# Slot attention and a rounded FFN on one core: a Newton step and the moves of the value states at other places, weight pieces at fixed points

## The chip, the cores and the metric

The kernel runs on one core of a Trainium2 chip. The metric is the device time of one execution in microseconds (us). The engines have short names: PE (TensorE, matmuls and transposes), DVE (VectorE), ACT (ScalarE), POOL (GpSimd) and SP (SyncE, which issues most DMAs). Each engine works through its own queue in order.

## What is computed

Four sequences (b = 0 to 3) of 512 tokens with 512 features go through an attention with slots and then through a feed-forward net (FFN) whose weights are rounded to fp8. Both read a layernormed input and add to the residual stream.

```python
# attention, 16 heads, DK = M = 64, DV = 128
q, k, v = x @ Wq, x @ Wk, x @ Wv                    # per head
s = clip(x @ Ws, -32, 32)                           # 64 slots per head
z = cumlogsumexp(s, axis=time); p = exp(s - z); g = exp(z_before - z)
hk[t] = hk[t-1] * g[t] + k[t] (x) p[t];  ok[t] = (q[t] * DK**-0.5) @ hk[t]
pv = softmax(ok)                                    # over the slots
hv[t] = hv[t-1] * g[t] + p[t] (x) v[t];  o[t] = pv[t] @ hv[t]
o = o * rsqrt(mean(o**2) + eps) * g_norm * silu(x @ Wg)
y = o @ Wo
# FFN, 1536 hidden
h = silu((x @ fp8(gate_w)) * gate_scale) * ((x @ fp8(up_w)) * up_scale)
y = (h @ fp8(down_w)) * down_scale
```

## The kernel before

**Units.** The 16 heads are taken in 8 groups g of two heads. A unit is one group of one sequence, written (g,b). The first 16 units have b = 0 and 1 (for each g first b = 0, then b = 1), the second 16 have b = 2 and 3. Even g also project the values of two groups (ps_v, 48 matmuls), so even units are longer. Where fp32 accuracy is wanted, a matrix is held in three parts (a high part, a low part, a corrected one) and a product is three passes of matmuls: 12 for a 128 x 512 result (L513, L550), 24 in four blocks for the output (L867).

**One unit** (`attention`, L950). On PE: slots ps_s, keys ps_k, queries ps_q; transposes of e (the exponentials of the clamped slot logits) and of k; in even units the values; transposes of the unit before's output (ps_oT, `turn_output`); ps_a (keys by queries within blocks of 64 tokens), ps_sk and ps_sv (states, `key_states` and `value_states`); the two gates ps_g; ps_ok (`slot_scores`, L697); then the unit before's output projection ps_o in shares of 6, 10, 4 and 4 matmuls, between which the softmax runs: transposes ps_okn of okT (L731), transposes ps_w of the exponentials (L775), ps_b (L780), and at last ps_ov (`read_states`, `read_within`). So the unit before's output is scaled, transposed, split and projected inside this one (object `before`).

**Names that the change touches.** z is the running sum of the slots' exponentials and rzT its reciprocal, first as exp(-ln z) on ACT (L661, L662) and then made exact by a Newton step on DVE (`inverse`, L664: L666 and L667). okT = ps_ok times rzT (L727, DVE) and wT = ps_w times rzT (L777, DVE). `turn_output` multiplies the transposed output with the gate (L846, DVE, sg); `high_output` rounds it on ACT (L852), `split_output` makes the other two parts on DVE (L856, L857). States of one half of the partitions are needed in the other half: `key_states` has three POOL operations for that (L685 to L687) and `value_states` four (L761 to L764); ps_ov reads the result, moved_v and svo. POOL's queue also issues the DMAs that add the output's rows to the residual stream in DRAM (L879), behind ACT's copy y of ps_o (L878), and has the small power operations (L339, L821).

**The list of work.** `work` is a Python list of small pieces that the program's author lets issue between a unit's own steps. In the first half these are the splits of the raw weights: ACT makes a high part (L260), DVE the other two (L266, L267), 512 columns at a time; the last piece of a matrix also starts a DMA that keeps it for the second half. A piece's high part is issued one step ahead of its rest. In the second half they are the rounding of the FFN's weights (`quantize`, in steps of two DVE operations each: L457 and L458, L464 and L465, L470 and L471, the last with a DMA). There are also pieces of the layernorm of later sequences (xn, xs). `other(n)` issues n entries (by default pace[0]), `piece()` issues up to the next whole piece, `need(key)` all entries up to the last one named key. `next_step` and `early_step` issue one transposing step of a layernorm. `load` starts the next unit's weights. What is issued where depends on g, b, on pace[0] and on what the list has at its head; `first_unit` writes the order of unit (0,0) out by hand. In ACT's queue, `exp_and_log` loads the table for exponentials and logarithms after the gates' Silu.

The order in which the engines get their instructions is the order of these calls; nothing is moved by a scheduler.

Of the kernel before, what the change touches and what calls it, by code (L numbers as in the profile page):

```python
# [40 lines left out]
AF = mybir.ActivationFunctionType  # L41
# [8 lines left out]
def kernel(  # L50
# [18 lines left out]
    nc = tc.nc  # L69
# [102 lines left out]

    pace = [1]

    def other(count=None):
        for _ in range(count or pace[0]):
            if work:
                work.pop(0)[1]()

# [114 lines left out]
    def next_step():  # L294
        if steps:
            steps.pop(0)()
# [328 lines left out]
    class Heads:  # L625


        def __init__(self, g, b):
            self.u, self.g, self.b = f"{g}_{b}", g, b
            self.v0 = g % 2 * HV  # L630
            self.sg = []
# [123 lines left out]
        def value_states(self):  # L755
            pts = states(self.e, both_v[self.b], self.v0, DV, f"ps_sv_{self.u}")
            self.sv = one.tile([P, NT - 1, DV], F32, tag="sv", name=f"sv_{self.u}")
            self.svo = svo = one.tile([P, NT, DV], F32, tag="svo", name=f"svo_{self.u}")
            add_up(svo, pts, self.sv)
            self.moved_v = moved = one.tile([P, NT, DV], F32, tag="kT", name=f"moved_v_{self.u}")  # L760
            nc.gpsimd.tensor_copy(moved[half(0), 1:, :], self.sv[half(1)])  # L761
            nc.gpsimd.tensor_copy(moved[half(1), 0, :], svo[half(0), 0, :])
            nc.gpsimd.tensor_tensor(moved[half(1), 1:, :], svo[half(0), 1:, :], self.sv[half(0)], ALU.add)
            nc.gpsimd.tensor_tensor(svo[half(1), 1:, :], svo[half(1), 1:, :], self.sv[half(1)], ALU.add)  # L764
# [70 lines left out]

        def gate(self, h):
            self.sg.append(one.tile([P, T], F32, tag=f"sg{h}", name=f"sg_{self.u}_{h}"))
            p = project("g", self.b, f"{'g'}_{self.u}_{h}", h * DV)
            nc.scalar.activation(self.sg[h], p, AF.Silu)

        def turn_output(self, h, n_bank=None):

# [40 lines left out]
    def exp_and_log():  # L883
        nc.scalar.preload_act_table_set("natural_log_exp_and_others")

    def first_unit():
# [11 lines left out]
        for _ in range(5):  # L898
            piece()
        transposing = layernorm(1, 1)  # L900
        work.extend(parts())
        load_matrix("g", 0, True)
        other(2)
        X.slots()
        other(2)
        X.keys()
        X.running_sum()
        other(2)
        X.queries()
        X.turn_e()  # L910
        X.turn_k()
        other(2)
        X.values(2)
        other(2)
        X.key_states()
        X.move_queries()
        X.inverse()
        X.values(3)
        fetch()
        fetch()  # L920
        load_matrix("o", 0, True)
        other(1)
        transposing()
        next_step()
        other(2)
        X.query_key()
        next_step()
        other(3)
        X.gate(0)
        X.slot_scores()  # L930
        X.value_states()
        next_step()
        X.softmax()
        X.softmax_exp()
        other(1)
        X.gate(1)
        exp_and_log()
        X.slot_weights()
        X.move_weights()
        next_step()  # L940
        X.weight_slot()
        need("xs_1")
        X.softmax_sum()
        need("xs_0")
        piece()
        X.read_states()
        X.read_within()
        return X

    def attention(g, b, before, load, gated):  # L950

        X = Heads(g, b)
        even = g % 2 == 0
        small = other if even or b > 1 or pace[0] > 1 else piece
        first = pace[0] > 1 and even and b == 1

        def early_step():

            if not any(name.endswith("_m") for name, _ in work):
                next_step()

        need(f"xs_{b}")
        need("s")
        X.slots()
        load("s")
        if not even:
            early_step()
        before.scale_output()  # L970
        need("k")

        X.keys()
        before.scale_other()
        X.running_sum()
        if not first:
            small()
        load("k")
        if not even:
            early_step()  # L980
        need("q")
        X.queries()
        if first:
            other(3)
        elif even or turned():
            other()
        load("q")
        X.turn_e()
        if even:
            X.turn_k()  # L990
            next_step()
            if turned():
                other(1)
            need("v")
            X.values(0)
            if first or b > 1:
                other(1)
            X.values(1)
            before.turn_output(0)
            before.high_output(0)  # L1000
            before.turn_output(1)
            before.high_output(1)
            other()
            X.values(2)
            before.split_output(0)
            next_step()
            other()
            X.values(3)
            before.split_output(1)
            next_step()  # L1010
        else:
            before.turn_output(0)
            X.turn_k()
            before.turn_output(1)
            before.high_output(0)
            before.high_output(1)
        X.query_key()
        X.key_states()
        X.value_states()
        X.move_queries()  # L1020
        if even:
            other()
        else:
            if b > 1:
                early_step()
            before.split_output(0)
            before.split_output(1)
        X.inverse()
        if work and work[0][0] == "o":
            other()  # L1030
        need("g")
        X.gate(0)
        if even:
            other()
            next_step()
        elif work and work[0][0] == "o":
            other()
        X.gate(1)
        exp_and_log()
# [24 lines left out]
        X.softmax_sum()  # L1064
        X.read_states()
        if even and b == 1 and not first and not turned():
            piece()
        elif even or b > 1 or steps:
            other()
# [105 lines left out]
    with tc.manual_schedule(engines=EVERY):  # L1175
# [17 lines left out]
        for i, (g, b) in enumerate(units[1:], 1):  # L1193
# [13 lines left out]

            def gated():

                pace[0] = 1 + (pace[0] > 1 and i > 1)  # L1210
# [20 lines left out]
            if b > 1:  # L1231
                for _ in range(min(0 if units[i] == (0, 2) else 2 if g % 2 else 4 if b == 2 else 3, to_come[0])):
                    work += [("round", f) for f in quantize()]
                    to_come[0] -= 1
            pace[0] = 2 if i == 1 or (g, b) in ((0, 2), (NG - 1, 0), (NG - 1, 2)) else 1
            if i == 1:
                pass
            elif g % 2:
                if b > 0 and not turned():
                    piece()  # L1240
                while work and work[0][0][:2] in ("xs", "xn") and b % 2:
                    other(1)
# [94 lines left out]
```

## Time and profile before

| | us |
|---|---|
| median of 3 runs | 1437.73 (1436.96 to 1437.81) |
| the profiled execution | 1438.3 |
| its span, first to last instruction | 1436.6 |
| granted TensorE clock, mean | 0.994 of full speed |

| stretch of the span, us | PE busy | DVE busy | ACT busy | POOL busy |
|---|---|---|---|---|
| 0 to 57.8, unit (0,0) | 50.42 | 42.64 | 27.86 | 15.52 |
| 57.8 to 590, rest of the first half | 512.16 | 369.96 | 305.88 | 172.85 |
| 590 to 1121, second half but its last unit | 518.58 | 398.61 | 275.79 | 171.93 |
| 1121 to 1160, unit (7,3) | 35.50 | 26.91 | 20.97 | 11.70 |
| 1160 to 1436.6, FFN | 271.21 | 117.61 | 73.90 | 14.38 |

Such tables are busy time by engine and stretch. Below, lines of a timeline read: start, duration, engine, line, operation, what is written and read, shapes, how many, and in brackets the idle time before it and what ended it. A line of the waits reads: engine and instruction, what it waited for, then the total, the number of waits and the longest one.

### The profile page before, as it was taken

How to read it: one execution, taken by the hardware profiler on the slowest of the kernel's cores; microseconds unless marked ns; L12 is line 12 of the kernel's file. 1: busy time of each engine (PE TensorE's matmuls, PEld its weight loads, DVE VectorE, ACT ScalarE, POOL GpSimd, SP SyncE). 2: the span in 40 equal slices, each digit the busy share in tenths (PEclk: the TensorE clock that was granted, in tenths of full speed). 3: DMA queues.
4: the chain of work that ended last, by engine and by line, in shares of the span. 5: the costliest groups of instructions: out<-in, count | busy, mean ns of one | idle time of the engine just before them, and what ended most of it. 6: DMA issues, size and time to landing. Idle time of an engine off the chain costs nothing.

```text
span 1436.6 us, 31108 instructions
## 1 busy us (share of the span) xinstructions
PE 1387.9 (97%) x13163; PEld 1108.3 (77%) x13163; DVE 955.7 (67%) x1625; ACT 704.4 (49%) x1329; POOL 386.4 (27%) x433
## 2 busy tenths in 40 slices
PE   8999899999999999999999999999999999999998
PEld 4687787778777877778777877877887788888886
DVE  6767657765786578667877887787778753435333
ACT  4556555655665555544545554455545543222221
POOL 2133323322332234332323341243224220000000
PEclk9999999999999999999999999999999999999999
DMA  8174655665565574546546664667465561101000
GB/s 337 67 242 141 184 143 177 185 201 162 164 188 173 153 235 126 140 140 205 170 119 178 213 173 121 184 199 208 109 184 170 154 184 23 59 1 59 0 30 29
DMA packets 80890, 213.04 MB, mean 148 GB/s; under 512 B 6168, under 2 KB 35120, under 8 KB 75568
## 3 DMA queue, kind: packets, MB, share of 16 engines
q1 hardware_dynamic: 62224, 177.49, 33.7%
q0 software_dynamic: 18528, 33.58, 15.7%
q8 instruction: 103, 1.69, 0.5%
q14 instruction: 35, 0.29, 0.1%
HBM read 107.23 MB, written 108.00 MB: 150 GB/s over the span
## 4 chain that ended last, share of the span: by engine, by line
PE 75%; DVE 18%; ACT 4%; issue 2%; POOL 0%; DMA 0%; DVEq 0%; ACTq 0%; POOLq 0%
PE ps_v L550 11%; PE ps_o L867 10%; PE ps_fg L1087 6%; PE ps_fu L1087 6%; PE ps_s L513 5%; PE ps_q L513 5%; PE ps_g L513 5%; PE ps_k L513 5%; PE ps_fd L1148 3%; PE ps_fe L1148 3%; DVE oT L857 2%; DVE sv L621 2%; PE ps_ov L796 2%; DVE z L666 2%; PE ps_ov L806 2%; PE ps_oT L565 2%
## 5 line engine op out<-in xcount | busy, mean ns | idle before, releaser
L867 PE MATMUL ps_o<-w_o,oT 128*128 128x512 f32 x768 | 213.7, 412 | 5.9 <-DVE w_o L267 4.7
L513 PE MATMUL ps_g<-xs,w_g 128*128 128x512 f32 x744 | 181.0, 399 | 0.0
L879 POOL DMA_DIRECT2D stream<-y x128 | 111.9, 874 | 222.1 <-ACT y L878 219.3
L550 PE MATMUL ps_v<-w_v,xs 128*128 128x512 f32 x720 | 171.5, 393 | 0.0
L513 PEld LDWEIGHTS ps_g<-xs,w_g 128*128 128x128 f32 x744 | 138.9, 190 | 33.9 <-issue 5.2
L867 PEld LDWEIGHTS ps_o<-w_o,oT 128*128 128x128 f32 x768 | 134.5, 189 | 36.0 <-DVE w_o L267 5.6
L550 PEld LDWEIGHTS ps_v<-w_v,xs 128*128 128x128 f32 x720 | 132.9, 188 | 26.2
L685 POOL COPY moved<-sk 64x192 f32<-64x192 f32 x32 | 11.2, 350 | 417.3 <-DVE sk L621 417.3
L1108 DVE SCALAR_TENSOR_TENSOR h<-ps_fu,scol,act 128x512 f32<-128x512 f32 x48 | 36.0, 751 | 113.7 <-PE ps_fu L1087 113.7
L846 DVE SCALAR_TENSOR_TENSOR sg<-ps_oT,scol,sg 128x512 f32<-128x512 f32 x64 | 46.4, 748 | 97.3 <-PE ps_oT L565 95.6
L878 ACT COPY y<-ps_o 128x512 f32<-128x512 f32 x128 | 74.5, 582 | 45.5 <-PE ps_o L867 44.8
L1087 PE MATMUL ps_fg<-xs,wf 128*128 128x512 f32 x384 | 95.7, 391 | 0.0
L1087 PE MATMUL ps_fu<-xs,wf 128*128 128x512 f32 x384 | 94.8, 389 | 0.0
L513 PE MATMUL ps_s<-xs,w_s 128*128 128x512 f32 x372 | 93.8, 401 | 0.0
L513 PE MATMUL ps_q<-xs,w_q 128*128 128x512 f32 x372 | 90.1, 391 | 1.6 <-DVE eT L638 1.6
L513 PE MATMUL ps_k<-xs,w_k 128*128 128x512 f32 x372 | 89.6, 390 | 0.0
L557 ACT COPY v<-ps_v 128x512 f32<-128x512 f32 x60 | 35.3, 588 | 102.2 <-PE ps_v L550 102.2
L821 POOL TENSOR_TENSOR rs<-rs,mhalf 128x8 f32<-128x8 f32 x32 | 58.3, 1823 | 99.1 <-DVE rs L818 87.7
L1087 PEld LDWEIGHTS ps_fu<-xs,wf 128*128 128x128 f32 x384 | 72.1, 188 | 15.0
L1087 PEld LDWEIGHTS ps_fg<-xs,wf 128*128 128x128 f32 x384 | 71.5, 188 | 14.9 <-issue 0.2
L513 PEld LDWEIGHTS ps_q<-xs,w_q 128*128 128x128 f32 x372 | 69.4, 188 | 17.1 <-issue 2.8
L513 PEld LDWEIGHTS ps_s<-xs,w_s 128*128 128x128 f32 x372 | 67.7, 189 | 18.0 <-issue 4.3
(168 smaller groups left out, 2870.6 us busy)
## 6 DMA issues: line engine op xcount, KB each, us to landing
stream<-y POOLq DMA_DIRECT2D x128, 256.0 KB, 4.9
split_v<-w_v SPq DMA_DIRECT2D x4, 3072.0 KB, 11.9
split_g<-w_g SPq DMA_DIRECT2D x8, 1536.0 KB, 7.9
split_o<-w_o SPq DMA_DIRECT2D x8, 1536.0 KB, 7.1
w_v<-split_v SPq DMA_DIRECT2D x4, 3072.0 KB, 16.2
w_g<-split_g SPq DMA_DIRECT2D x8, 1536.0 KB, 6.9
w_o<-split_o SPq DMA_DIRECT2D x8, 1536.0 KB, 8.6
rounded<-qw SPq DMA_DIRECT2D x36, 256.0 KB, 4.3
```

The source lines that it names most:

```text
L513: nc.tensor.matmul(p, wt[self.nm][:, j, at : at + P], xs[self.b][i][:, c, :], start=(i == 0 and c == 0), stop=(i == 2 and c == KC - 1),)
L550: nc.tensor.matmul(p, xs[b][i][:, c, n * P : (n + 1) * P], wt["v"][:, j, c * 2 * HV : (c + 1) * 2 * HV], start=(i == 0 and c == 0), stop=( ...
L557: nc.scalar.copy(to, p)
L565: nc.tensor.transpose(pt[:, n, :], s, by)
L821: nc.gpsimd.tensor_tensor(rs, rs, mhalf.rearrange("p (h n) -> p h n", h=HG), ALU.pow)
L846: nc.vector.scalar_tensor_tensor(self.sg[h], pt.rearrange("p n t -> p (n t)"), gw, self.sg[h], ALU.mult, ALU.mult,)
L867: nc.tensor.matmul(self.p, self.oT[:, i, h, n * P : (n + 1) * P], wt["o"][:, j, h * D : (h + 1) * D], start=(i == 0 and h == 0), stop=(i = ...
L878: nc.scalar.copy(y, self.p)
L879: nc.gpsimd.dma_start(stream[self.b][n * P : (n + 1) * P, :], y, accum_op=ALU.add)
L1087: nc.tensor.matmul(pp, w[:, c * P : (c + 1) * P], xs[b][k][:, c, :], start=(c == 0 and k == 0), stop=(c == KC - 1 and k == 1),)
L1108: nc.vector.scalar_tensor_tensor(h, pu, us, act, ALU.mult, ALU.mult)
L1148: nc.tensor.matmul(sums[n], parts[k][:, n * P : (n + 1) * P], fw[c][2], start=(c == 0 and k == 0), stop=(c == NFC - 1 and k == 1),)
```

## The change

It has four parts.

1. `inverse` issues right after the transposes of e (odd units) or of k (even units), before `turn_output`, and no longer after `move_queries`.
2. The four POOL operations of `value_states` become `move_states`, which issues after `slot_scores` and the first six matmuls of the output projection, so behind the first stream DMA on POOL's queue.
3. The pieces of `work` are issued by a new `fill(count)` at fixed places of a unit, the same for all even and all odd units but for b < 2: one whole piece, or one entry in the second half, and then a high part that is at the list's head. The places that depended on pace[0], and the pieces ahead of each unit, go. Unit (0,1) issues the remaining parts of the first sequence's input, xs_0, before its ps_a.
4. In unit (0,0) the slots' clamp, the Newton step and ps_a come earlier, both gates leave PSUM only after ps_b (so that one pair of ACT's table loads goes), and the parts of xs_0 and the split of w_o move to unit (0,1).

PE's, DVE's, POOL's and SP's instructions are the same ones in another order; ACT has two fewer, both loads of a function table. PE's order changes in unit (0,0) alone.

```diff
@@ class Heads
+        def move_states(self):
+            svo = self.svo
             self.moved_v = moved = one.tile([P, NT, DV], F32, tag="kT", name=f"moved_v_{self.u}")
             nc.gpsimd.tensor_copy(moved[half(0), 1:, :], self.sv[half(1)])
...
         def gate(self, h):
-            p = project("g", self.b, f"{'g'}_{self.u}_{h}", h * DV)
-            nc.scalar.activation(self.sg[h], p, AF.Silu)
+            self.pg[h] = project("g", self.b, f"{'g'}_{self.u}_{h}", h * DV)
+        def gate_silu(self, h):
+            nc.scalar.activation(self.sg[h], self.pg.pop(h), AF.Silu)
@@ new
+    def fill(count):
+        for _ in range(count):
+            if pace[0]:
+                piece()
+            else:
+                other(1)
+        if work and work[0][0] in ("s_", "k_", "q_", "g_", "v_", "o_"):
+            other(1)
@@ first_unit
         X.turn_k()
+        X.inverse()
         other(2)
         X.values(2)
         other(2)
+        X.query_key()
         X.key_states()
         X.move_queries()
-        X.inverse()
...
         X.value_states()
+        X.move_states()
...
         X.weight_slot()
+        X.gate_silu(0)
+        X.gate_silu(1)
+        exp_and_log()
         need("xs_1")
         X.softmax_sum()
-        need("xs_0")
-        piece()
         X.read_states()
         X.read_within()
+        work.extend(later)
+        load_matrix("o", 0, True)
@@ attention
+        pace[0] = b < 2
...
         X.running_sum()
-        if not first:
-            small()
         load("k")
...
+        fill(1 if b < 2 else 2)
         need("q")
         X.queries()
-        if first:
-            other(3)
-        elif even or turned():
-            other()
         load("q")
         X.turn_e()
         if even:
             X.turn_k()
+            X.inverse()
             next_step()
-            if turned():
-                other(1)
             need("v")
             X.values(0)
-            if first or b > 1:
-                other(1)
+            fill(1)
             X.values(1)
...
             before.high_output(1)
-            other()
+            fill(1)
             X.values(2)
             before.split_output(0)
             next_step()
-            other()
+            fill(1)
             X.values(3)
             before.split_output(1)
             next_step()
+            fill(1)
         else:
+            X.inverse()
             before.turn_output(0)
...
+        if units[1] == (g, b):
+            need(f"xs_{b - 1}")
         X.query_key()
         X.key_states()
         X.value_states()
         X.move_queries()
-        if even:
-            other()
-        else:
+        if not even:
             if b > 1:
-                early_step()
+                turning(True)
             before.split_output(0)
             before.split_output(1)
-        X.inverse()
-        if work and work[0][0] == "o":
-            other()
+            fill(1)
         need("g")
...
         X.slot_scores()
         before.project_output(6)
+        X.move_states()
         X.softmax()
         X.softmax_exp()
-        if even and b == 1 and not first and not turned():
-            piece()
-        elif not turned():
-            small()
-        elif not even and b > 1:
-            other(1)
+        fill(1)
         before.project_output(10)
...
-        small()
         X.softmax_sum()
+        if even or b > 1:
+            fill(1)
         X.read_states()
-        if even and b == 1 and not first and not turned():
-            piece()
-        elif even or b > 1 or steps:
-            other()
+        fill(1)
@@ the loop over units
-            pace[0] = 2 if i == 1 or (g, b) in ((0, 2), (NG - 1, 0), (NG - 1, 2)) else 1
-            if i == 1:
-                pass
-            elif g % 2:
-                if b > 0 and not turned():
-                    piece()
-                while work and work[0][0][:2] in ("xs", "xn") and b % 2:
-                    other(1)
-                if (g, b) == (NG - 1, 1):
-                    load_tokens(3, x)
-            else:
-                other(1 if b > 1 else 2)
+            if (g, b) == (NG - 1, 1):
+                load_tokens(3, x)
             before = attention(g, b, before, load, gated)
```

More of the change, by code (lines that the diff above doesn't have):

```diff
@@ L173, with other @@
     pace = [1]
-    def other(count=None):
-        for _ in range(count or pace[0]):
+    def other(count=1):
+        for _ in range(count):
             if work:
@@ L630, in __init__ @@
             self.v0 = g % 2 * HV
-            self.sg = []
+            self.sg, self.pg = [], {}
             self.left = [(n, i, j, h) for n in range(NT) for i, j in PAIRS for h in range(HG)]
@@ L884, in exp_and_log @@
         nc.scalar.preload_act_table_set("natural_log_exp_and_others")
+    def fill(count):
+        for _ in range(count):
+            if pace[0]:
[4 more added lines that the diff above has]
+            other(1)
     def first_unit():
@@ L897, in first_unit @@
         X.values(1)
-        for _ in range(5):
+        for _ in range(4):
             piece()
+        X.slots()
         transposing = layernorm(1, 1)
-        work.extend(parts())
+        later = parts()
         load_matrix("g", 0, True)
-        other(2)
-        X.slots()
         other(2)
@@ L920, in first_unit @@
         fetch()
-        load_matrix("o", 0, True)
-        other(1)
         transposing()
@@ L925, in first_unit @@
         other(2)
-        X.query_key()
+        X.gate(0)
         next_step()
-        other(3)
-        X.gate(0)
+        other(1)
         X.slot_scores()
         X.value_states()
+        X.move_states()
         next_step()
@@ L936, in first_unit @@
         X.gate(1)
-        exp_and_log()
         X.slot_weights()
@@ L955, in attention, with turning @@
         even = g % 2 == 0
[L956 to L961, printed above, removed]
+        pace[0] = b < 2
+        def turning(ready=False):
+            if not ready or not any(name.endswith("_m") for name, _ in work):
                 next_step()
@@ L975, in attention @@
         X.running_sum()
-        if not first:
-            small()
         load("k")
         if not even:
-            early_step()
+            turning(True)
+        fill(1 if b < 2 else 2)
         need("q")
         X.queries()
-        if first:
-            other(3)
-        elif even or turned():
-            other()
         load("q")
@@ L1020, in attention @@
         X.move_queries()
-        if even:
-            other()
-        else:
+        if not even:
             if b > 1:
-                early_step()
+                turning(True)
             before.split_output(0)
             before.split_output(1)
-        X.inverse()
-        if work and work[0][0] == "o":
-            other()
+            fill(1)
         need("g")
         X.gate(0)
+        X.gate_silu(0)
         if even:
-            other()
             next_step()
-        elif work and work[0][0] == "o":
-            other()
         X.gate(1)
+        X.gate_silu(1)
         exp_and_log()
@@ L1062, in attention @@
         load("o")
-        small()
         X.softmax_sum()
+        if even or b > 1:
+            fill(1)
         X.read_states()
-        if even and b == 1 and not first and not turned():
-            piece()
-        elif even or b > 1 or steps:
-            other()
+        fill(1)
         if even:
@@ L1208, in gated @@
             def gated():
-                pace[0] = 1 + (pace[0] > 1 and i > 1)
                 if g == NG - 2 and b % 2 == 1:
@@ L1234 @@
                     to_come[0] -= 1
-            pace[0] = 2 if i == 1 or (g, b) in ((0, 2), (NG - 1, 0), (NG - 1, 2)) else 1
-            if i == 1:
-                pass
-            elif g % 2:
-                if b > 0 and not turned():
-                    piece()
-                while work and work[0][0][:2] in ("xs", "xn") and b % 2:
-                    other(1)
-                if (g, b) == (NG - 1, 1):
-                    load_tokens(3, x)
-            else:
-                other(1 if b > 1 else 2)
+            if (g, b) == (NG - 1, 1):
+                load_tokens(3, x)
             before = attention(g, b, before, load, gated)
```

## The prediction, made before the changed kernel was run

> **What bounds the kernel now.** I read the engines' totals first, then PE's waits, then the timelines of one unit. All times are us; the profiled execution took 1438.3, its span is 1436.6.
>
> ```profile
> PE 1387.9 (97%) x13163; PEld 1108.3 (77%) x13163; DVE 955.7 (67%) x1625; ACT 704.4 (49%) x1329; POOL 386.4 (27%) x433
> ```
>
> PE is the bound, idle for 1436.6 - 1387.9 = 48.7. The change leaves PE's instructions as they are, so 48.7 caps any gain, and everything turns on which PE waits go and which come. PE's waits:
>
> ```profile
> PE ps_okn L565 <- DVE okT L727: 17.9, 17, 1.3
> ...
> PE ps_o L867 <- DVE w_o L267: 4.7, 2, 2.4
> PE ps_b L586 <- DVE wT L777: 3.9, 7, 0.9
> ...
> PE ps_sv L607 <- DVE xs L368: 1.8, 1, 1.8
> ...
> PE ps_q L513 <- DVE eT L638: 1.6, 3, 0.5
> ```
>
> (Total, times, longest.) One wait dominates: the transposes ahead of the softmax want okT. Unit (3,2) shows why it is late; DVE, then POOL, then PE:
>
> ```profile
> 827.70 0.68 DVE L856 TENSOR_TENSOR oT<-sg,oT 128x512 fp32r<-128x512 f32 x1
> 828.42 0.88 DVE L857 SCALAR_TENSOR_TENSOR oT<-oT 128x512 fp32r<-128x512 f32 x1
> 829.22 0.77 DVE L856 TENSOR_TENSOR oT<-sg,oT 128x512 fp32r<-128x512 f32 x1
> 830.02 1.38 DVE L857 SCALAR_TENSOR_TENSOR oT<-oT 128x512 fp32r<-128x512 f32 x1
> 831.33 1.50 DVE L666 SCALAR_TENSOR_TENSOR z<-z,rzT 128x512 f32<-128x512 f32 x1
> 832.86 0.69 DVE L667 SCALAR_TENSOR_TENSOR rzT<-z,rzT 128x512 f32<-128x512 f32 x1
> 833.66 0.76 DVE L727 TENSOR_TENSOR okT<-ps_ok,rzT 128x256 f32<-128x256 f32 x2
> ```
> ```profile
> 828.20 0.55 POOL L761 COPY moved_v<-sv 64x384 f32<-64x384 f32 x1 [0.57 <-PE ps_g L513]
> 828.80 0.64 POOL L762 COPY moved_v<-svo 64x128 f32<-64x128 f32 x1
> 829.41 1.44 POOL L763 TENSOR_TENSOR moved_v<-svo,sv 64x384 f32<-64x384 f32 x1
> 830.93 1.34 POOL L764 TENSOR_TENSOR svo<-svo,sv 64x384 f32<-64x384 f32 x1
> ```
> ```profile
> 831.52 1.66 PE L867 MATMUL ps_o<-w_o,oT 128*128 128x512 f32 x6
> 834.47 0.66 PE L565 MATMUL ps_okn<-idents,okT 128*128 128x128 f32 x4 [1.29 <-DVE okT L727]
> 834.88 2.57 PE L867 MATMUL ps_o<-w_o,oT 128*128 128x512 f32 x10
> ```
>
> The Newton step (L666, L667) stands between the split of the output (L856, L857) and okT. And DVE and POOL hold each other up: L857 takes 1.38 beside L763, L666 1.50 beside L764, each ending .55 after the POOL row, where they take .69 alone (L667 here). With no wait the transposes would start 1.50 after ps_o's first matmul, at 833.02: a cost of 1.45 with the restart of the pipeline.
>
> The Trainium skill, "SBUF — State Buffer" (sections "🔬 SBUF: two separate sides" and "Who interferes with whom"), calls this an exclusive lock between a GpSimd operation and a DVE operation with two SBUF inputs or in a two-port mode; "Issue order, not op shape, decides who blocks." The two rows above agree with it. It speaks against the change: the four moves now meet the splits and roundings of the softmax gap, which have two SBUF inputs. By the rule, if a move always went first, wT would come .55 later (L761's row) in some 30 units, 16 more in the sum; by the rows, where pieces and moves alternate, the sum is the one below.
>
> **The change part by part.** Call O the start of ps_o's first six matmuls.
>
> *Newton before the output's transposes, moves after slot_scores (odd units).* Newton's input rzT is there when it now issues, in the shadow of the transposes. It makes sg, and with it a, sk and the key moves on POOL (behind sk), .5 to .7 later; the cover is the gate's 24 matmuls (5.74 in unit (1,0)). If that cover were gone the loss would be .5 in each of 16 units. In (3,2) the split would start .4 later (828.2, since sv comes later) but, no longer meeting L761 to L764, take 4 x .69 and end at 831.0; one fill piece (two operations of .42 to .69) and okT (.76) follow, to end between 832.6 and 833.15, where 833.02 is wanted. So the stall goes but for some .1: 1.45 in each of six late odd units and 1.4 in (7,2), 1.35 in (3,0), (5,0), (3,1), (5,1) and (7,0), and 2.5 over six late even units, which lose .2 to .7 here, where two operations fewer stand before okT: 8.7 + 1.4 + 6.75 + 2.5 = **19.4** (the waits alone are 17.9 of the view above; bounds 10 and 21). (1,0) is counted below.
>
> *The moves' new place.* On POOL they stand behind the first stream DMA (.90, issued at O + 2.58). They run from O + 3.55; alone .55 + .3 + 1.0 + 1.0 gives O + 6.7 with gaps; beside DVE pieces, by the rows above, 4.3 and O + 7.9. ps_ov reads moved_v at O + 7.69. I take 6.7, no wait; the other end is .2 in each of 31 units, 6. Behind the moves on POOL wait the next stream DMAs, for which nothing near waits. On DVE, mx, ok, wT read PSUM, and such rows (okT beside L764, .42 each) were not lengthened. Of the fill pieces a rounding pair (L457, L458, .42 each) ends at O + 4.8 and a split pair at O + 5.34; wT's transposes end at O + 5.1. So 0 to .14 late; I take 0.
>
> *Units (2,1), (4,1), (6,1).* Here the piece's ACT half (L260, .61) runs behind the exponential, so L266 starts at O + 4.95, between two moves: blocked behind L763, then L267 behind L764, wT 2.3 late against 1.1 now. Loss 3 x 1.2 = **3.6** (bounds 0 and 6).
>
> *Other waits that go.* (Bounds 0 and 7.) The .5 waits of ps_q for eT in (4,0) and (6,0), .7 with restart: 1.4. ps_b in (3,1) and (5,1): 1.3. ps_sv in (0,2): 1.5 of 1.8, since the xs parts come earlier. (1,1) and (0,3): .4. Together **4.6**.
>
> *First unit.* The clamp issues before the v pieces: the .9 of ps_q <- eT goes. Two table loads of ACT go (1.28 each in unit (1,0)); of their 2.56 I take 1.9, as PE has other work for part of it. Gain **2.8** (0 to 5).
>
> *Early units, where pieces come later than before* (bounds 4 and 15 together). (0,1): both w_o pieces now stand right before okT, and their ACT halves behind the gate's table load. By (1,0)'s rows ACT is free at 118.2; .61, then four DVE operations at .69 and .76 for okT give 122.3, against 118.7 wanted: 3.6. Its w_s piece, behind the exponential like those above but without their present wait: 2.3. Loss **5.9**. (1,0): the last piece of w_g comes behind the split. Newton adds 1.4 to DVE there, the split ends at 117.4, the piece at 118.8; ps_g starts at 110.9 and can run 6 of 12 matmuls, to 112.3. Wait 6.0 to 6.5; less the okn stall and a kn wait that go (1.8), loss **4.2**. (2,0): w_q's piece behind z, ps_q waits 1.1 instead of .7: **.4**. (7,1): two pieces of w_o before okT against xs parts moved away: 0 (bounds -2.4 and +.7).
>
> *The end of the attention.* With fewer rounding pieces per unit, 16 DVE operations of rounding are left between rs of (7,3) and the FFN's first h. Today nothing stands there:
>
> ```profile
> 1160.04 0.17 DVE L818 SCALAR_TENSOR_TENSOR rs<-rs,sq 128x8 f32<-128x8 f32 x1
> 1161.66 0.75 DVE L1108 SCALAR_TENSOR_TENSOR h<-ps_fu,scol,act 128x512 f32<-128x512 f32 x1 [1.46 <-PE ps_fu L1087]
> ```
> ```profile
> 1163.21 1.98 PE L1087 MATMUL ps_fu<-xs,wf 128*128 128x512 f32 x8
> ```
>
> Seven at .42 and nine at .69 make 9.2, so h ends at 1160.2 + 9.2 + .75 = 1170.2. The second ps_fu needs the bank that h frees: 7.0 late, **7.0** (bounds 3 and 9). In (7,3) Newton stands before xn, which PE waits for already: **1.15**.
>
> **Sum.** Gains 19.4 + 4.6 + 2.8 = 26.8; losses 3.6 + 5.9 + 4.2 + .4 + 7.0 + 1.15 = 22.25. 1438.3 - 4.55 = 1433.75 for such an execution; the median of the runs, 1437.73, is .57 below it, so **1433.2**.
>
> **Rivals.**
> *A: the late pieces cost little.* If DVE catches up in (0,1), (1,0) and before the FFN (two thirds of 17.1 gone, and the 3.6), 1433.2 - 11.4 - 3.6 = 1418. For: DVE is busy 67%. Against: the backlog is in the issue order, and an engine can't pass its own queue.
> *B: the softmax becomes the bound.* The moves hold DVE up between ok and wT in nearly every unit, so that ps_b and then ps_ov wait. Price: one POOL move more before wT, .8 in 30 units, 24: 1457. It decides once the fill piece ends later than O + 5.1, when wT's transposes are done. For: the 1.38 and 1.50 above. Against: the moves start only as ok ends, and pieces alternate with them.
> *C: early units and the end cost more than I count.* Their upper bounds (2.4 in (7,1), 2 in the FFN, 2.4 in the three units, 4 more in the first half) give 1444.
> *D: no effect.* Stalls return elsewhere one for one; 1437.7. Against: the 19.4 is made of waits with nothing late behind them.
>
> **How the numbers follow.** A measurement can tell some .2% from no change: 1434.9 to 1440.6 is "the same". Forecast .42 (1427 to 1439; .32 of it under 1434.9, .10 above), A .2, B .12, C .18, D .08. Faster: .32 + .2 = .52; the same: .10 + .08 and .02 of C = .20; slower: .12 + .16 = .28. The likeliest's own range is 1427 to 1439; 1417 to 1446 takes in C, D and most of A and leaves out B and the tails, some .16.
>
> **What would show it.** Right: in late odd units okn idles under .2 and L857 takes .69; ps_ov has no new wait for moved_v; ps_g of (1,0) waits some 6 for w_g; ps_fu at the FFN's start waits some 7 for h. Wrong: a row of ps_b <- wT with 25 times or more (B), or no wait of DVE's at 1163 (A).

## The result, and the profile after

The changed kernel took 1453.64 us (median of 4 runs, 1449.29 to 1455.44), the kernel before 1437.77: a ratio of 1.0106, 95% interval 1.0083 to 1.0130. It is slower by 1.1%, where 1433.2 was forecast. Its profiled execution took 1449.3, the lowest of the four, with a span of 1447.6 and a mean granted clock of 0.985 (before: 1436.6 and 0.994). Where the other three lost some 3 to 6 us more no trace shows; their clocks were 0.983 and 0.984.

PE's waits in the changed kernel (total, times, longest), with lines as in the view of before:

```profile
PE ps_xn L352 <- DVE xn L343: 9.3, 7, 3.5
PE ps_fu L1086 <- DVE h L1107: 6.3, 1, 6.3
PE ps_o L872 <- ACT y L883: 6.0, 4, 4.8
PE ps_q L513 <- DVE eT L638: 5.5, 1, 5.5
PE ps_g L513 <- DVE w_g L267: 5.4, 1, 5.4
PE ps_b L586 <- DVE wT L780: 4.3, 4, 1.3
PE ps_o L872 <- ACT w_o L260: 3.9, 3, 1.5
PE ps_o L872 <- DVE w_o L267: 2.7, 4, 0.8
...
PE ps_okn L565 <- DVE okT L727: 0.4, 1, 0.4
```

The wait that bounded the units, 17.9 us of ps_okn for okT, is gone but for 0.4. In its place stand a few long waits. Two of them the prediction had (ps_fu, ps_g); ps_q for eT and ps_o for y it did not have. One more line has grown: ps_xn for xn, 4.7 before, now 9.3; 1.8 of it is in unit (7,1), 1.2 at the end of (0,0) and 0.9 in (0,2).

Taken by units on PE (from the start of one ps_s to the next, both profiled executions), the 11.0 us between the spans are:

| units | change, us | forecast, us |
|---|---|---|
| (0,0) | -4.2 | -2.8 |
| odd units (3,0) to (7,0) and (1,2) to (7,2), even units from (2,2) on; with the ps_b waits of (3,1) and (5,1) | -20.4 | -20.7 |
| (4,0), (6,0), (0,2), (0,3) | -2.5 | -3.1 |
| (2,1), (4,1), (6,1) | +2.9 | +3.6 |
| (0,1) | +6.1 | +5.9 |
| (1,0) | +13.3 | +4.2 |
| (1,1) | +6.1 | -0.2 |
| (2,0), (7,1) | +2.0 | +0.4 |
| (7,3) and the FFN | +7.5 | +8.15 |

Gains came to 27.1 (forecast 26.8), losses to 37.9 (forecast 22.25); the start was 0.2 later. Of the difference of 15.6 between forecast and profiled execution, (1,0) and (1,1) make 15.4; the errors of the other rows cancel to 0.2. What ACT did there, in the timeline:

```profile
98.69 0.42 ACT L751 ACTIVATE sq<-sm 64x4 f32<-64x4 f32 x2
100.13 0.63 ACT L260 ACTIVATE w_q<-raw_q 128x512 fp32r<-128x512 f32 x1 [1.02 <-DMA raw_q<-in_L_attn_Wq_dram]
107.67 0.63 ACT L260 ACTIVATE w_g<-raw_g 128x512 fp32r<-128x512 f32 x1 [6.90 <-DMA raw_g<-in_L_attn_Wg_dram]
108.20 1.07 ACT L819 ACTIVATE og<-ps_ov 128x512 f32<-128x512 f32 x2
...
175.62 0.63 ACT L260 ACTIVATE w_k<-raw_k 128x512 fp32r<-128x512 f32 x1 [4.48 <-DMA raw_k<-in_L_attn_Wk_dram]
176.16 0.57 ACT L883 COPY y<-ps_o 128x512 f32<-128x512 f32 x1
```

At the end of (0,1) `fill` issues a high part of w_g ahead, and ACT stands 6.90 us at it, since the raw weights have not landed. Behind it in ACT's queue are the squares of ps_ov (L819), behind these rs and then eT on DVE, and ps_q waits for the buffer that eT's clamp frees: 5.5 us. In (1,1) the same happens with w_k and the copy y of ps_o: 4.8 us. In the kernel before, ACT has not one such wait. SP's queue shows why the weights are late:

```profile
95.54 0.37 SPq L218 DMA_DIRECT2D raw_q<-in_L_attn_Wq_dram  x1
95.95 0.50 SPq L277 DMA_DIRECT2D split_s<-w_s  x1
99.62 0.37 SPq L218 DMA_DIRECT2D raw_g<-in_L_attn_Wg_dram  x1
100.03 0.62 SPq L277 DMA_DIRECT2D split_k<-w_k  x1
```

In the kernel before, the load of raw_g is

```profile
80.19 0.37 SPq L218 DMA_DIRECT2D raw_g<-in_L_attn_Wg_dram  x1
```

A load is issued when one of the two raw buffers comes free, that is when a matrix has been split; raw_g is issued at 99.62 and lands 8.0 us later, beside the stores of splits. Before, it was issued at 80.19 and landed 4.0 us later.

### The profile page after: what moved, and what is told of

Its sections match the earlier page's. It is cut to its first block, busy times and chain, and to the rows that moved or that the text cites. A ratio compares the mean times of both kernels' runs of the same rounds, so it can differ in the third digit from the quotient of the medians.

```text
span 1447.6 us, 31071 instructions
## 1 busy us (share of the span) xinstructions
PE 1392.4 (96%) x13163; PEld 1115.2 (77%) x13163; DVE 911.1 (63%) x1625; ACT 703.0 (49%) x1327; POOL 356.6 (25%) x433
## 3 DMA queue, kind: packets, MB, share of 16 engines
q0 software_dynamic: 18528, 33.58, 15.4%
## 4 chain that ended last, share of the span: by engine, by line
PE 89%; DVE 6%; DMA 2%; ACT 2%; issue 1%; POOL 0%; SPq 0%; DVEq 0%; ACTq 0%; POOLq 0%
PE ps_g L513 12%; PE ps_o L872 12%; PE ps_v L550 11%; PE ps_fu L1086 6%; PE ps_fg L1086 6%; PE ps_s L513 6%; PE ps_k L513 5%; PE ps_q L513 5%; PE ps_fd L1147 3%; PE ps_fe L1147 3%; PE ps_ov L799 2%; PE ps_ov L809 2%; PE ps_sv L607 2%; PE ps_oT L565 2%; PE ps_b L586 1%; PE ps_a L586 1%
## 5 line engine op out<-in xcount | busy, mean ns | idle before, releaser
L872 PE MATMUL ps_o<-w_o,oT 128*128 128x512 f32 x768 | 218.7, 418 | 12.5 <-ACT y L883 6.0
L513 PEld LDWEIGHTS ps_k<-xs,w_k 128*128 128x128 f32 x372 | 69.7, 188 | 14.5
L1113 ACT CAST both<-h 128x512 fp32r<-128x512 f32 x48 | 29.8, 620 | 104.8 <-DVE h L1107 104.8
## 6 DMA issues: line engine op xcount, KB each, us to landing
split_v<-w_v SPq DMA_DIRECT2D x4, 3072.0 KB, 11.5
w_v<-split_v SPq DMA_DIRECT2D x4, 3072.0 KB, 15.6
```

What stands on the lines that cost most here:

```text
L513: nc.tensor.matmul(p, wt[self.nm][:, j, at : at + P], xs[self.b][i][:, c, :], start=(i == 0 and c == 0), stop=(i == 2 and c == KC - 1),)
L872: nc.tensor.matmul(self.p, self.oT[:, i, h, n * P : (n + 1) * P], wt["o"][:, j, h * D : (h + 1) * D], start=(i == 0 and h == 0), stop=(i = ...
L1113: nc.scalar.copy(hi, h)
```

## The experiments

Unless a table says otherwise, a time is a median, and the ratio is to the kernel before, run on the same chip.

**Parts 1 and 2 alone.** b_newton moves only `inverse`, b_moves only `move_states`, b_both both, in the kernel before with its own places for pieces.

```diff
+            X.inverse()          # after turn_k (even), before turn_output (odd)
...
-        X.inverse()
...
         before.project_output(6)
+        X.move_states()
```

> The kernel before with the Newton step and the moves of the value states at their new places, and nothing else of the change. Theory L (the loss is in the first units, where weight pieces come later than the loads allow, and the late rounding; the new places themselves gain): the okT waits of 17.9 us go, ps_b waits stay near 4, about 1419 us (1416 to 1423). Rival K (the moves in the softmax gap hold DVE up): ps_b <- wT waits in 20 units or more, 1436 us or more.

> The kernel before with the Newton step at its new place, the moves of the value states where they were. If the moves in the softmax gap make the ps_b waits of b_both (11.3 us in 8 waits, with the clock falling behind some), those stay near before's 3.9 here; the okT waits go all the same, since 2.2 us of DVE leave the queue ahead of okT and only 1.45 are missing: 1418 to 1424 us, and a narrow spread. If the lock between POOL and the split was the larger part, okT waits of 6 us or more stay: 1428 or more.

> The kernel before with the moves at their new place and the Newton step where it was. If each part alone is enough for okT (split and Newton unblocked take 1.7 us less), okT waits fall under 4 us, but the ps_b waits are b_both's, 10 to 12 us: 1427 to 1434 us. If the Newton step is needed as well, okT waits stay at 10 us or more: 1436 or more.

| kernel | us | ratio, 95% | okT waits, us | ps_b waits, us |
|---|---|---|---|---|
| b_newton | 1417.20 | 0.9864 (0.9842 to 0.9886) | none | 3.9 in 7 |
| b_moves | 1422.20 | 0.9897 (0.9881 to 0.9913) | none | 11.4 in 8 |
| b_both | 1431.57 | 0.9953 (0.9936 to 0.9970) | none | 11.3 in 8 |

Each part alone removes the okT waits; both together gain less than either. b_newton and b_moves came in under their ranges, b_moves by 5 us. b_both missed its 1419: the moves cost something in the softmax gap, though in 8 waits and not in the 20 units that rival K asks for. b_moves has the same ps_b waits and is 9.4 faster. What b_both has besides is four waits of ps_sk for sg, 4.1 us, which the Newton step delays (b_newton has them too), and more stretches of a lowered clock. Unit (3,1) of b_both, DVE, then POOL, then PE:

```profile
293.84 0.69 DVE L736 TENSOR_TENSOR ok<-ps_okn,mx 128x512 f32<-128x512 f32 x1
295.75 1.00 DVE L266 TENSOR_TENSOR w_s<-raw_s,w_s 128x512 fp32r<-128x512 f32 x1 [1.22 <-ACT w_s L260]
296.78 1.38 DVE L267 SCALAR_TENSOR_TENSOR w_s<-w_s,raw_s 128x512 fp32r<-128x512 f32 x1
298.08 0.68 DVE L780 TENSOR_TENSOR wT<-ps_w,rzT 128x512 f32<-128x512 f32 x1
```
```profile
295.20 1.00 POOL L766 TENSOR_TENSOR moved_v<-svo,sv 64x384 f32<-64x384 f32 x1
296.27 1.33 POOL L767 TENSOR_TENSOR svo<-svo,sv 64x384 f32<-64x384 f32 x1
```
```profile
298.82 0.69 PE L586 MATMUL ps_b<-wT,eT 64*64 64x64 f32 x32 [1.84 <-DVE wT L780]
299.44 1.88 PE L870 MATMUL ps_o<-w_o,oT 128*128 128x512 f32 x4
```

The piece starts 1.22 late, since its high part stood behind ACT's exponential; then L266 and L267 take 1.00 and 1.38 instead of 0.69 beside two moves. And the four ps_o matmuls after the wait take 1.88, where the four before it took 1.31: the granted clock was 0.50 from 300 to 302 (more below).

**The late high part.** b_both_ahead is b_both with this before slot_scores:

```diff
         need("o")
+        if b < 2 and work and work[0][0].endswith("_"):
+            other(1)
```

> b_both, with the high part at the head of the list issued before slot_scores in the first half, ahead of ACT's exponential. Theory M (the moves cost only where a split piece starts late, since its high part stands behind the exponential, and then meets them): the ps_b waits fall from 11.3 to under 4 us, the clock stays over 0.99, 1414 to 1421 us. Rival K (the moves hold DVE up in the softmax gap by themselves): ps_b waits of 8 us or more stay, 1427 or more.

1412.78, ratio 0.9825 (0.9806 to 0.9844); ps_b waits 1.9. It is 18.8 below b_both (the kernel before stood at 1437.94 beside b_both and at 1438.00 beside this one). Theory M holds: with the moves in the same place, ps_b waits fall from 11.3 to 1.9 when the piece starts in time.

**The early units.** a_late_high keeps `fill` from issuing a high part ahead at three places, a_raw3 gives the raw weights a third buffer, a_first takes before's `first_unit`, a_xs0 only does the parts of xs_0 at the end of the first unit again.

```diff
# a_late_high
+        fill(1, (g, b) != (1, 1))                 # after softmax_exp
+        fill(1, (g, b) not in ((0, 1), (1, 1)))   # after read_states
# a_raw3
-            tag = f"raw{fetched[0] % 2}"
+            tag = (("raw0", "raw1") * 2)[fetched[0]] if fetched[0] < 4 else ("qw", "raw0", "raw1")[(fetched[0] - 4) % 3]
...
         scale_columns()
+        fetch()
# a_xs0
         X.softmax_sum()
+        for _, run in later:
+            run()
         X.read_states()
         X.read_within()
-        work.extend(later)
...
-        if units[1] == (g, b):
-            need(f"xs_{b - 1}")
```

> The changed kernel, but the last fill of units (0,1) and (1,1) and the softmax's fill of (1,1) issue no high part ahead. Theory L (ACT stands at a high part whose raw weights have not landed, with the squares of ps_ov and the copy y of ps_o behind it): the waits ps_q <- eT 5.5 and ps_o <- y 4.8 go, and with them the fall of the granted clock in units (1,0) and (1,1): 10 to 15 us less than the changed kernel, some 1438 to 1442. Rival S (the pieces are late whatever ACT does, DVE waits in its place): under 4 us less.

> The changed kernel with a third buffer for raw weights (the one that held the scales), so that each load is issued one matrix earlier; the order of all other instructions stays. Theory D (in (1,0) and (1,1) ACT stands at high parts whose loads were issued too late, and the clock falls behind that): ps_q <- eT falls from 5.5 to under 2 and ps_o <- y from 4.8 to under 1, and 8 to 14 us go: 1440 to 1446. Rival S (the DVE operations put into (0,1) delay the pieces whatever the loads do): under 4 us go, and the same PE waits come back at DVE's pieces.

> The changed kernel with the first unit of before, so that the parts of xs_0 and the split of w_o come before unit (0,1) again. Theory L: the first unit loses its gain of 4.2, units (0,1), (1,0), (1,1) lose some 20 of their 25 us of loss, no granted clock under 0.95 there: 1430 to 1437 us. Rival S (the fixed places of fill are at fault whatever the first unit does): the three units stay within 8 us of the changed kernel's 129.8, 1447 us or more.

> The changed kernel with the four parts of xs_0 back at the end of the first unit; w_o's split stays in unit (0,1). Theory L1 (the eight DVE operations put into (0,1) push every weight piece back): units (0,1) to (1,1) lose some 20 us of their excess, the first unit or the start of (0,1) pays 1 to 4: 1428 to 1434 us. Rival L2 (w_o's split in (0,1) is what pushes): under 8 us less than the changed kernel, 1442 or more.

| kernel | us | ratio, 95% | (0,0) | (0,1) | (1,0) | (1,1) | (2,0) |
|---|---|---|---|---|---|---|---|
| changed | 1453.64 | 1.0106 (1.0083 to 1.0130) | -4.2 | +6.1 | +13.3 | +6.1 | +0.1 |
| a_late_high | 1446.50 | 1.0067 (1.0042 to 1.0093) | -4.2 | +5.3 | +9.1 | 0.0 | +5.8 |
| a_raw3 | 1438.02 | 1.0002 (0.9992 to 1.0012) | -4.2 | +6.0 | +7.0 | 0.0 | +0.1 |
| a_xs0 | 1428.56 | 0.9941 (0.9925 to 0.9957) | -4.2 | +3.9 | -1.8 | -0.9 | +0.1 |
| a_first | 1424.66 | 0.9917 (0.9895 to 0.9940) | -1.2 | +0.8 | -1.7 | -5.2 | +1.3 |

(Units: us against the kernel before, in one profiled execution each. The same first unit took 0.1 more than before's in b_newton and 1.2 less in clock_dose, so a_first's -1.2 is no gain.) a_late_high gained 7.1, between what the theory and its rival asked: the waits left (1,1) and (1,0)'s ps_q and came back in (2,0) as ps_q for w_q. a_raw3 decides between its theory (late loads) and its rival (late pieces, whatever the loads do). With the same order of instructions but for the loads it is 15.6 faster by the medians, more than was expected, and 10.4 by the profiled executions, of which the changed kernel's is its fastest; (1,0) and (1,1) lose 12.4 of their excess. raw_g is now issued at 94.89, and ACT's wait for it shrinks from 6.90:

```profile
100.92 0.63 ACT L260 ACTIVATE w_g<-raw_g 128x512 fp32r<-128x512 f32 x1 [1.82 <-DMA raw_g<-in_L_attn_Wg_dram]
```

and the waits of ps_q for eT and of 4.8 for y are gone. What is left in (1,0) is w_g's last piece behind the split, 5.3 us of ps_g, as forecast. a_xs0 shows where the lateness begins: without the four parts of xs_0 in (0,1), eight DVE operations, (1,0) is faster than before. What they take is mostly places of `fill`. In a_xs0 w_o's two pieces and w_s's first stand behind sg and between the output's splits, at 74.64, 77.30 and 79.96; in the changed kernel three parts of xs_0 stand there (70.47, 73.12, 75.79), and w_o's pieces come at 85.27 and 86.60, right before okT. The eight operations themselves are only 5.5 us of DVE. w_o's split in (0,1), the other step of part 4 that went there, did little harm by itself. a_first came in under its range: the three units after the first are 31.5 shorter than in the changed kernel, where 20 were expected.

**The FFN's start.** a_tail issues one rounding entry more at three places of the even units of the third sequence.

```diff
-            fill(1)
+            fill(2 if b == 2 else 1)
```

> The changed kernel with one rounding entry more at three places of the even units of the third sequence, so that no rounding is left at the FFN's start. If the 16 late operations are the cause of the wait of ps_fu for h (6.3 us), it goes and 6 to 8 us with it, with nothing lost in the units that got more: 1442 to 1447 us beside 1449 to 1455. If the even units have no room on DVE for it, okT or wT waits of 2 us or more appear there and the gain is under 3.

1443.10, ratio 1.0049 (1.0032 to 1.0065), 10.5 below the changed kernel; (7,3) and the FFN go from +7.5 to -0.3, and no even unit of the third sequence gets longer by more than 0.1 for it. The 16 operations were the cause of that wait. Unit (0,2) is 1.1 shorter, as its wait of 0.9 for xn is gone too. The rest of the medians' difference, some 1.6, can't be placed from one profile of each.

**Better versions.** a_best1 is a_first with a_tail's edit and `if b < 2: fill(0)` after `need("o")`, which issues only a high part at the list's head; a_best1_moves puts `move_states` back behind `value_states`; a_best3 has a_best1's other edits with the changed first unit, in which it does xs_0's four parts where DVE is idle; a_best3_raw3 adds the third buffer.

> a_first with a_tail's rounding entries, and the high part at the head of the list issued before slot_scores in the first half, so that it is not behind the exponential. Theory: 6 to 7 us of the ps_fu wait and 1.5 to 2 in each of (2,1), (4,1), (6,1) go: 1411 to 1415 us. If the ps_b waits of these units come from the moves and not from the late high part, they stay: 1417 or more.

> a_best1 with the moves of the value states back behind the value states. Theory: with the Newton step gone from the stretch before okT the moves' place is worth nothing where pieces start in time: within 2 us of a_best1's 1407.5. If the unblocked split is needed as well, because fill puts a piece between it and okT: okT waits of 5 us or more and 1413 us or more.

> The changed kernel with the parts of xs_0 in idle stretches of DVE within the first unit, w_o's split in (0,1) as changed, a_tail's rounding entries and the high part ahead as in a_best1. If the first unit's gain and the weight pieces' time can both be had: first unit 35.7 to 36.5, (0,1) 39.5 to 41, (1,0) 28.7, 1403 to 1407 us. If the parts hold up the first unit's own chain, it takes 38 us or more and the kernel is no faster than a_best1.

> a_best3 with the third buffer. Its pieces wait for loads only in (2,0) (ps_q <- w_q 2.0) and little else: 1401 to 1404 us; no change if that wait is DVE's order alone.

| kernel | us | ratio, 95% |
|---|---|---|
| a_best1 | 1407.47 | 0.9794 (0.9776 to 0.9811) |
| a_best1_moves | 1424.27 | 0.9913 (0.9897 to 0.9930) |
| a_best3 | 1404.46 | 0.9773 (0.9757 to 0.9789) |
| a_best3_raw3 | 1403.02 | 0.9758 (0.9743 to 0.9772) |

a_best1 is under its range; (2,1), (4,1) and (6,1) go from +1.0 to -1.0 each, so that in the changed order too the late high part was the cause of their ps_b waits. a_best3 and a_best3_raw3 can't be told apart by these intervals. a_best1_moves fell against its theory: the place of the moves is worth 16.8 here, though b_newton did without it. `fill` puts a piece between the split and okT. In unit (3,2), with the moves back at their old place, it meets them:

```profile
819.00 1.49 DVE L470 SCALAR_TENSOR_TENSOR q<-q,qw 128x512 f32<-128x512 f32 x1
820.52 1.39 DVE L471 SCALAR_TENSOR_TENSOR qw<-q 128x512 f32<-128x512 f32 x1
821.84 0.74 DVE L727 TENSOR_TENSOR okT<-ps_ok,rzT 128x256 f32<-128x256 f32 x2
```
```profile
818.48 1.46 POOL L766 TENSOR_TENSOR moved_v<-svo,sv 64x384 f32<-64x384 f32 x1
820.01 1.35 POOL L767 TENSOR_TENSOR svo<-svo,sv 64x384 f32<-64x384 f32 x1
```

The rounding pair takes 2.9 instead of a_best1's 1.4, and okT waits of 11.5 us in 11 units are back. So part 2 pays for the piece that part 3 puts there. a_best3's gain over a_best1 is in the first unit (-4.2 against -1.2) and (0,1) (-0.4 against +0.8); (1,0) and (1,1) give 0.8 and 0.9 of it back.

**The price of a wait.** clock_dose is b_newton with reductions on DVE between ok and wT in twelve units; their result is overwritten.

```diff
+            for _ in range(EXTRA.get((self.g, self.b), 0)):   # 2 to 5
+                nc.vector.tensor_reduce(
+                    self.sm, self.okT.rearrange("p (n m) -> p n m", m=M), AX.X, ALU.max
+                )
```

> b_newton with 2 to 5 reductions (some 0.67 us each, result overwritten) between ok and wT on DVE in twelve units of the second half, so that ps_b waits for a known time. If a wait of PE costs only itself: each unit is longer by its ps_b wait and no more, granted clock 0.99 or more. If a wait of some 1.5 us or more makes the granted clock fall for a while, as in units (3,1) and (5,1) of b_both: units with 4 or 5 reductions are longer by 1 to 4 us beyond the wait, those with 2 are not.

1441.91, ratio 1.0032 (1.0019 to 1.0045). Beside b_newton, in the ten units with 2 to 4 reductions ps_b started 1.06 to 2.18 later, and the unit grew by that and no more, to 0.1. In the two with 5, (2,3) and (5,2), it started 3.22 and 2.56 later, and the unit grew by 4.75 and 4.07: 1.5 more each. So a wait can make the clock fall and cost more than its length. In this kernel 4 reductions did nothing, but no bound on the length follows: in b_moves a wait of 1.30 with one of 0.38 ahead of it did it (last section).

## Why the prediction was wrong

**Newton's and the moves' gain: right.** 20.4 against 20.7 in the odd and late even units. Unit (3,2) of the changed kernel, DVE, then PE:

```profile
839.34 1.11 DVE L862 SCALAR_TENSOR_TENSOR oT<-oT 128x512 fp32r<-128x512 f32 x1
842.41 0.69 DVE L471 SCALAR_TENSOR_TENSOR qw<-q 128x512 f32<-128x512 f32 x1
843.02 0.75 DVE L727 TENSOR_TENSOR okT<-ps_ok,rzT 128x256 f32<-128x256 f32 x2
```
```profile
842.98 1.66 PE L872 MATMUL ps_o<-w_o,oT 128*128 128x512 f32 x6
844.47 0.60 PE L565 MATMUL ps_okn<-idents,okT 128*128 128x128 f32 x4
```

The transposes start 1.49 after ps_o's first matmul, as forecast, and without a wait. One thing was not foreseen: one L862 (L857 before) still takes 1.11, beside the last move of the keys (L687, 838.62 to 839.89), which now comes 0.5 later in the unit; it costs PE nothing here. That either part alone is enough the prediction did not say.

**Softmax gap: right for the changed kernel, in three units.** Wait and price in (2,1), (4,1), (6,1) were foreseen (2.9 against 3.6), with the mechanism, which b_both_ahead and a_best1 then showed. Rival B was wrong for the changed kernel (4 ps_b waits, not 25), but moves that hold DVE up cost b_both 14.4 beside b_newton, the lowered clock counted in.

**The end of the attention: right in the wait, helped by chance in the sum.** The 16 operations are there; ps_fu waited 6.3 where 7.0 was forecast, and (7,3) with the FFN lost 7.5 against 8.15. But the eight matmuls behind that wait took 3.67 instead of 1.98 (the granted clock is 0.50 there), which no term had, and xn's wait in (7,3) stayed at 3.5, where the Newton step was to add 1.15 (it shows as 0.45 of ps_sk for sg).

**First unit: right, less the clock.** 4.2 against 2.8, but a_first, with before's order of that unit, took 1.2 less than before's own profiled execution, whose granted clock there was 0.98 and not 1.00. That leaves 3.0. Which of the edits gave how much was not tried.

**Unit (0,1): the number right by luck.** 6.1 against 5.9. The forecast was 3.6 for okT behind w_o's pieces and 2.3 for w_s's piece. PE's waits there are 2.8 for w_o itself, 0.3 for wT and none for okT; the other 3 us come with a granted clock of 0.93, which no term had.

**Unit (7,1): a term put at nothing.** +1.9 where 0 (at most +0.7) was forecast, with a new wait of ps_xn for xn of 1.8.

**Early units: the step that failed.** The terms for (1,0) and (1,1), 4.2 and -0.2, became 13.3 and 6.1. The prediction priced pieces there by DVE and ACT alone: "ACT is free at 118.2; .61, then four DVE operations". It left out, and so put at nothing, that a piece has a DMA ahead of it. The parts of xs_0 in (0,1) put off each split, each split puts off the issue of a later load, and a high part then stands on ACT with the unit's own squares and copies behind it. Of (1,0)'s 13.3, 6.3 go with a_raw3, and all of (1,1)'s 6.1; the 7.0 left in (1,0) are the forecast 4.2 and the clock. The prediction followed the moved steps through POOL's and DVE's queues, and ACT's only for the table load and the exponential, not behind a load. Rival C had the early units and the end cost more, but named no cause, and its bounds (4 more in the first half) end at 1444, too cheap. Rival A, that late pieces cost little, failed in the same units.

**The clock: left out.** No term had it. In units (0,1), (1,0) and (1,1) PE's waits make 20.7 us in the changed kernel and 5.0 before; the units grew by 25.4. So nearly 10 us are not waits. There the granted clock is 0.93, 0.84 and 0.87, after 0.99, 1.00 and 0.95 before. The wait for w_g in (1,0) of the changed kernel, on PE:

```profile
119.24 1.65 PE L513 MATMUL ps_g<-xs,w_g 128*128 128x512 f32 x6
126.26 6.80 PE L513 MATMUL ps_g<-xs,w_g 128*128 128x512 f32 x18 [5.37 <-DVE w_g L267]
```

As forecast, six matmuls run and the rest wait; but the other 18 then take 6.80, where all 24 took 5.74 before, so some 2.5 more. The same 20.2 us from the span's start, before, then after, where unit (1,0) starts at 97.6 and at 99.8 (PE, PEld, DVE, ACT and POOL busy with counts, granted clock, DMA share, GB/s):

```profile
99.80:120.00 20.20, 18.78 (x222) 15.08 (x220) 15.39 (x25) 13.18 (x24) 8.60 (x9) 1.00 0.32 114
```
```profile
99.80:120.00 20.20, 14.69 (x145) 12.01 (x144) 10.79 (x20) 9.88 (x21) 1.67 (x1) 0.83 0.57 185
```

The granted clock, 1.00 before, is 0.83 there, part of it while PE is idle, which costs nothing. a_raw3 has the same slow 18 matmuls (6.98) behind the same wait.

## What to carry to other kernels

Where a step is moved, follow its resources back to the load: the piece, the buffer whose release issues the load, the load's landing, and what stands on the waiting engine behind it. A list that is emptied at fixed places is a queue: one addition at its head makes everything behind it late, and the price appears several matrices later. Two edits that each remove the same wait do not add up, and one of them can be what pays for a third.

## What was not expected of the hardware

**A long wait of PE costs more than its length.** clock_dose, unit (2,3), PE, then stretches:

```profile
798.73 1.17 PE L872 MATMUL ps_o<-w_o,oT 128*128 128x512 f32 x4
803.05 0.69 PE L586 MATMUL ps_b<-wT,eT 64*64 64x64 f32 x32 [3.15 <-DVE wT L782]
803.67 2.07 PE L872 MATMUL ps_o<-w_o,oT 128*128 128x512 f32 x4
```
```profile
802.00:804.00 2.00, 0.95 (x33) 0.89 (x34) 1.20 (x3) 0.94 (x3) 0.00 (x0) 0.91 1.12 426
804.00:806.00 2.00, 2.00 (x12) 1.16 (x15) 2.00 (x6) 0.67 (x2) 0.84 (x1) 0.50 1.24 350
806.00:809.00 3.00, 3.00 (x63) 2.72 (x56) 0.89 (x3) 1.56 (x6) 0.86 (x1) 0.83 0.76 206
```

Four matmuls take 2.07 instead of 1.17, and the granted clock is 0.50. The missing clock of the three stretches, 0.18 + 1.0 + 0.51 us, makes 3.4 us at half. In b_both a wait of 1.84 (unit (3,1), above) was followed by the same, while the same 1.84 in (1,1) was not, and b_both's runs spread over 1425.9 to 1434.1. So the length alone doesn't decide.

The phase does. In each of the 16 traces all changes of the granted clock lie on one grid of 3.41 us, to 3 ns. b_moves has the same two waits (0.38 and 1.30) in (2,1) and (4,1); its grid cuts them differently, and only (4,1) loses the clock:

```profile
235.56:238.97 3.41, 2.23 (x52) 1.71 (x56) 2.57 (x6) 1.76 (x4) 1.32 (x2) 1.00 0.60 79
238.97:242.39 3.42, 3.42 (x61) 2.91 (x54) 2.02 (x4) 2.37 (x7) 1.18 (x2) 1.00 0.79 128
375.49:378.90 3.41, 1.72 (x36) 0.85 (x34) 2.74 (x3) 1.33 (x4) 2.36 (x3) 1.00 0.57 73
378.90:382.32 3.42, 3.42 (x40) 2.54 (x36) 2.64 (x5) 1.91 (x6) 1.23 (x2) 0.50 0.69 90
```

PE is busy for 2.23 of one stretch and for 1.72 of the other. Counted over all 16 traces, from 12 us on and for stretches at full clock: PE busy for under 0.43 of a stretch, the clock was halved for the next in 40 of 40; from 0.43 to 0.63, in 34 of 79; above, in none of 6378. Why the middle is mixed is not shown.

The Trainium skill, "TensorE: Matmul & The Clock Gate" (section "🔬 Part 1: The HAM clock gate (the "warmup" mystery)"), says that the clock has two states, full and half, decided over a free-running window of some 3.4 us. The 0.50 and the 3.41 above agree. It also gives as its rule that PE shouldn't idle for longer than some 3.4 us; here two waits of 0.38 and 1.30 close together were enough, and the measurement decides. That the phase also makes the spread between executions is likely, but with one trace per kernel it is not shown.

**Loads beside stores.** On SP's queue raw_k (256 KB) landed in 3.4 us when issued at 88.09 and in 9.7 when issued at 165.88. Ahead of the first that queue had issued nothing for 20 us, ahead of the second the store of split v (3 MB) 2.5 us before. That the store is the cause is likely and was not tried. A high part ahead that is safe in one unit is not in another.
